# Graph attention on one Trainium2 core: another start for the first two graphs, and the second group's row statistics on ScalarE

## The chip, the cores and the metric

The kernel runs on one core of a Trainium2 chip. Five engines of that core work side by side: TensorE (PE, matrix products; its weight loads are shown apart as PEld), VectorE (DVE), ScalarE (ACT), GpSimd (POOL) and SyncE (SP, which issues nearly all DMA transfers). Each engine carries out its own list of instructions strictly in order, and engines wait for one another through semaphores. The metric is device time in microseconds for the whole computation, the median over several runs; lower is better.

## The reference, cut to what matters

The inputs are 128 graphs of 128 nodes with 768 features, one 128x128 adjacency matrix for each graph, and three 768x768 weights. Everything is float32.

```python
h = relu(layernorm(x))                                  # over the 768 features
q, k, v = (split_heads(h @ W + b) for W, b in ...)      # 12 heads of 64
s = q @ k.T / 8 + beta * adj
s = where(adj > 0, s, -9e15)
x = x + merge_heads(softmax(s) @ v)
```

## The kernel before, in words

The function `direct` treats the graphs in 32 groups of four (`GRP`); `G` is the group and `g` the graph in it. Before the products of a group, each graph's x is normalised and transposed, so that the features lie on the partitions. The weights of all three projections stay in SBUF and are cut into three slices: `qk0` (queries and keys of heads 0 to 5), `v`, and `qk1` (heads 6 to 11).

**Products.** A slice of a group is one 2x3x3 block product made with 15 instead of 18 block products (`PRODUCTS`, `product`, L320 to L363). Sums of activation blocks (`sum_acts`, L283) and of weight blocks (`sum_weights`, L197) are made by VectorE. The 15 products are spread over four PSUM banks, the chains a, b, c and d; a product adds onto what its bank holds, so the next product of a chain may start only when the last one has been read out. The first product that reaches a result is read out by ScalarE (L357) for `qk` slices, and by VectorE (L347) for `v`; every later one is added by VectorE (L361, L352). Products 0, 2, 6, 9 and 12 are on chain c, 1, 5, 10 and 13 on chain a, 3, 7, 11 and 14 on chain b, and 4 and 8 on chain d.

**Order.** Work of other kinds (the scores, the weighted sums, the next group's preparation) is put between the products by lists `todo`, whose entries `then(n, f)` are called behind the n-th product. A scheduler then sets the final place of every instruction on its engine, and `tc.issue_after` keeps an instruction behind another one. The engines run in exactly the order that results.

**Preparing a group.** The usual way lays x out so that VectorE's 32x32 transposes (`to_hT`, L275) yield the feature blocks. Statistics: VectorE makes mean and variance of each 192-wide quarter row (`stats`, L230); in `moments_1` (L235) two small TensorE products sum the quarters' means over partitions and VectorE takes deviations; in `moments_2` (L251) two more such products (L255) sum the variances, VectorE adds the constant (L258, L260), and POOL takes the inverse root (L262) and the shift (L264). Then ScalarE normalises the sixteen quarter rows of the group one by one (`norm`, L273), and VectorE transposes them.

**Group 0** is different. Graphs 0 and 1 are loaded by rows. `rows_1` (L522) makes their row statistics on VectorE and the inverse root on POOL (L536); `rows_2` (L539) normalises three pieces of 256 columns on VectorE (L544), transposes each by two TensorE products with the identity (L549), and lets ScalarE move it to SBUF (L554). `WARM` products of the identity (L560) run on TensorE before that. The slice `qk0` of group 0 is made plainly with 18 block products (`plain_slice`, L485), the very first block graph by graph. Graphs 2 and 3 go the usual way in three steps (`half`, L577).

**Group 1** is prepared while the `v` slice of group 0 runs: x is loaded (L155) behind the weights of `qk1`, `stats` is called behind products 0 to 3, `moments_1` behind 5, `moments_2` behind 7, `norm` behind 10 to 13. Then comes the `qk1` slice of group 0, with the scores of heads 0 to 5 (L382) behind its product 1, their exponentials (L389) and the transposes of group 1 (L280).

## Time and profile before

| what | value |
|---|---|
| median of four runs | 2892.67 us (2892.52 to 2893.04) |
| the profiled execution's own time | 2892.54 us |
| its span, first to last instruction | 2890.8 us |
| TensorE busy | 2879.6 us, 100% of the span |
| VectorE, ScalarE, POOL busy | 1962.1, 801.9 and 371.5 us |
| the chain that ended last | 98% TensorE |

All times inside the span count from its first instruction. A row of the timeline gives the start, the length, the engine, the line, the operation, what is written and read, the shapes and how many instructions are merged; behind it, in brackets, stands how long the engine sat idle and what ended that. TensorE's rows are pipelined: products that are 379 ns long start closer together than that, so the space between starts tells what one costs.

### The profile page before, as it was taken

How to read it: one execution, taken by the hardware profiler on the slowest of the kernel's cores; microseconds unless marked ns; L12 is line 12 of the kernel's file. 1: busy time of each engine (PE TensorE's matmuls, PEld its weight loads, DVE VectorE, ACT ScalarE, POOL GpSimd, SP SyncE). 2: the span in 40 equal slices, each digit the busy share in tenths (PEclk: the TensorE clock that was granted, in tenths of full speed). 3: DMA queues.
4: the chain of work that ended last, by engine and by line, in shares of the span. 5: the costliest groups of instructions: out<-in, count | busy, mean ns of one | idle time of the engine just before them, and what ended most of it. 6: DMA issues, size and time to landing. Idle time of an engine off the chain costs nothing.

```text
span 2890.8 us, 81358 instructions
## 1 busy us (share of the span) xinstructions
PE 2879.6 (100%) x35562; PEld 2021.3 (70%) x35562; DVE 1962.1 (68%) x4743; ACT 801.9 (28%) x1750; POOL 371.5 (13%) x304
## 2 busy tenths in 40 slices
PE   9999999999999999999999999999999999999999
PEld 7666677666677676776667766777666777666766
DVE  7876667676676666767667776667666676666765
ACT  2432322222222323223232232322223222322221
POOL 1111111111111111111111111111111111111110
PEclk9999999999999999999999999999999999999999
DMA  6322122221122111221112212122221222111211
GB/s 166 78 56 57 38 62 71 60 56 43 55 71 64 52 52 46 71 68 51 56 42 68 71 52 60 39 63 71 55 61 39 58 71 61 56 47 47 67 41 39
DMA packets 357784, 172.16 MB, mean 60 GB/s; under 512 B 84400, under 2 KB 357040, under 8 KB 357424
## 3 DMA queue, kind: packets, MB, share of 16 engines
q1 hardware_dynamic: 355552, 166.53, 21.1%
q8 instruction: 279, 4.57, 0.7%
q10 hardware_dynamic: 1872, 0.40, 0.1%
q14 instruction: 81, 0.66, 0.1%
HBM read 116.53 MB, written 50.33 MB: 58 GB/s over the span
## 4 chain that ended last, share of the span: by engine, by line
PE 98%; issue 1%; DVE 1%; POOL 0%; ACT 0%; DMA 0%; SPq 0%; ACTq 0%; POOLq 0%; DVEq 0%
PE bank L336 84%; PE bank L417 6%; PE bank L382 6%; PE bank L498 1%; PE bank L560 0%; ACT x L273 0%; POOL rstd L262 0%; DMA x<-in_x_dram 0%; DVE S L286 0%; DVE qk L361 0%; PE bank L241 0%; PE bank L255 0%; PE bank L437 0%; DVE qk_T L206 0%; PE bank L454 0%
## 5 line engine op out<-in xcount | busy, mean ns | idle before, releaser
L336 PE MATMUL bank<-S,qk_T 128*64 128x256 f32 x7056 | 822.5, 379 | 0.9 <-ACT qk L357 0.8
L336 PEld LDWEIGHTS bank<-S,qk_T 128*64 128x64 f32 x7056 | 503.6, 137 | 256.8 <-issue 4.0
L361 DVE TENSOR_TENSOR qk<-qk,bank 128x512 f32<-128x512 f32 x630 | 428.9, 681 | 340.1 <-PE bank L336 337.2
L357 ACT ACTIVATE qk<-bank,bqk 128x256 f32<-128x256 f32 x756 | 312.2, 472 | 1009.5 <-PE bank L336 778.4
L336 PE MATMUL bank<-A,qk_T 128*64 128x256 f32 x4032 | 478.6, 379 | 0.9 <-DVE qk L361 0.9
L336 PE MATMUL bank<-S,qk_B 128*64 128x256 f32 x4032 | 478.2, 379 | 1.0 <-DVE qk L361 1.0
L422 POOL TENSOR_TENSOR xo<-xo,o 128x512 f32<-128x512 f32 x189 | 252.6, 1336 | 1599.2 <-DVE o L401 1364.1
L336 PE MATMUL bank<-v_T,S 128*64 128x256 f32 x3584 | 422.6, 380 | 0.0
L352 DVE TENSOR_TENSOR v<-v,bank 128x512 f32<-128x512 f32 x320 | 220.1, 688 | 295.9 <-PE bank L336 295.9
L389 ACT ACTIVATE e<-e 128x512 f32<-128x512 f32 x378 | 227.3, 631 | 660.4 <-DVE e L386 660.0
L336 PEld LDWEIGHTS bank<-A,qk_T 128*64 128x64 f32 x4032 | 284.3, 137 | 137.4 <-DVE qk L361 1.1
L336 PEld LDWEIGHTS bank<-S,qk_B 128*64 128x64 f32 x4032 | 278.6, 137 | 128.9 <-DVE qk L361 1.4
L336 PEld LDWEIGHTS bank<-v_T,S 128*64 128x64 f32 x3584 | 252.2, 137 | 126.3 <-issue 5.7
L273 ACT ACTIVATE x<-x,shift,rstd 128x192 f32<-128x192 f32 x504 | 224.3, 533 | 350.2 <-POOL shift L264 350.2
L336 PE MATMUL bank<-v_B,S 128*64 128x256 f32 x2048 | 244.1, 380 | 0.0
L386 DVE SCALAR_TENSOR_TENSOR e<-bank,biasT 128x512 f32<-128x512 f32 x378 | 231.3, 681 | 16.7 <-PE bank L382 16.7
L336 PE MATMUL bank<-v_T,A 128*64 128x256 f32 x2048 | 237.9, 379 | 0.0
L417 PEld LDWEIGHTS bank<-v,e 128*64 128x64 f32 x6048 | 208.6, 138 | 27.3
L280 DVE STREAM_TRANSPOSE A<-x 128x256 f32<-128x256 f32 x378 | 211.9, 612 | 4.0 <-ACT x L273 4.0
L417 PE MATMUL bank<-v,e 128*64 128x65 f32 x6048 | 208.3, 221 | 0.0
L347 DVE TENSOR_TENSOR v<-bv_b,bank 128x512 f32<-128x512 f32 x192 | 131.9, 687 | 111.9 <-PE bank L336 111.9
L230 DVE BATCH_NORM_STATS2 st<-x 128x6 f32<-128x192 f32 x504 | 154.4, 344 | 75.5 <-DMA x<-in_x_dram 75.5
(83 smaller groups left out, 1689.6 us busy)
## 6 DMA issues: line engine op xcount, KB each, us to landing
x<-in_x_dram SPq DMA_DIRECT2D x504, 96.0 KB, 2.5
xo<-in_x_dram SPq DMA_DIRECT2D x189, 256.0 KB, 2.9
out_dram<-xo SPq DMA_DIRECT2D x189, 256.0 KB, 2.4
adj<-in_adj_dram SPq DMA_DIRECT2D x128, 64.0 KB, 2.4
qk_T<-in_L_gnn_Wq_dram SPq DMA_DIRECT2D x10, 128.0 KB, 3.8
qk_T<-in_L_gnn_Wk_dram SPq DMA_DIRECT2D x10, 128.0 KB, 3.8
v_T<-in_L_gnn_Wv_dram SPq DMA_DIRECT2D x5, 256.0 KB, 6.1
qk_B<-in_L_gnn_Wq_dram SPq DMA_DIRECT2D x8, 128.0 KB, 3.5
```

Source lines behind the costliest of these rows:

```text
L230: nc.vector.bn_stats(st[G][:, g * NB + b, :], xg[G, g][:, b, :])
L273: nc.scalar.activation(t, t, AF.Relu, bias=shift[G, n], scale=rstd[G, n])
L280: last = nc.vector.transpose(t[:, :, g * N:(g + 1) * N].rearrange("p c (b i) -> p c b i", i=SQ), src)
L336: nc.tensor.matmul(p[q:q + HD, i, :], lhs[:, q:q + HD], rhs, start=(first and i == 0 and c == 0), stop=(c == 1), skip_group_check=True)
L352: added[G] = nc.vector.tensor_tensor(o, o, got, ALU.add if sign > 0 else ALU.subtract)
L357: nc.scalar.activation(t[:, i, :], p[:, i, :], AF.Identity, bias=bqk[:, i, oc:oc + 1], scale=float(sign))
L361: added[G] = nc.vector.tensor_tensor(t, t, p, ALU.add if sign > 0 else ALU.subtract)
L382: nc.tensor.matmul(ps[oc, i][k:k + HD, g * N:(g + 1) * N], t[r, 1, at][:, k:k + HD], t[r, 0, at], start=True, stop=True)
L386: taken[0] = nc.vector.scalar_tensor_tensor(e, ps[oc, i].rearrange("p (g n) -> p g n", g=GRP), SCORE_CAP * ISCALE, biasT[G], op0=ALU.min, ...
L389: nc.scalar.activation(e, e, AF.Exp, scale=1.0 / ISCALE)
L417: nc.tensor.matmul(pa[q:q + HD, 2 * g + i, :], es[G, oc, i][:, 2 * r + g, q:q + HD], vt[G, "v", r, h // 4][:, 4 * g + h % 4, :], start=Tru ...
L422: nc.gpsimd.tensor_add(t, t, o.rearrange("p a (b j) d -> p (a b) (j d)", j=2))
```

## The change

Three things change, all of them at the start of the kernel.

*Graphs 0 and 1.* `rows_1` and `rows_2` are replaced by `begin` and `transposed`. On VectorE the second graph's statistics now stand between the first graph's pieces, one by one. On TensorE a fixed order is written out by `line` and `PIECES`: the transposes of a piece stand just ahead of the products that need it, or one piece earlier, and this for both graphs. `WARM` stays 18. On POOL, the scaling of `beta_c` and a memset now stand ahead of the second graph's inverse root.

*Statistics of group 1.* In place of `stats` on VectorE, `stats_by_act` has ScalarE go over each quarter row twice: a copy with a sum output gives the mean, a square with the mean as bias and a sum output gives the variance. It works on graphs 0 and 1 (called behind product 8 of the plain slice) and then on graphs 2 and 3 (called behind product 0 of the `v` slice). The first-half entries are then copied for `moments_1`, which reads two halves. The four `norm` calls are asked for one product earlier.

*Loads.* x of the first two graphs of group 1 is loaded ahead of the `qk1` weights, and not behind them.

In the order that results, ScalarE has its 32 passes between the read-outs of the plain slice and up to the normalising of group 1, and the square of `adjT` (L311) now stands ahead of that normalising. On TensorE the two small products of `moments_1` move from the middle of product 10 of the `v` slice to behind half of product 12, and those of `moments_2` from behind the first instruction pair of product 12 to behind the first pair of product 14. VectorE loses sixteen statistics instructions in that slice; from its last sum of the slice on, its order is the same as before.

```diff
--- before.py
+++ after.py
@@ -228,6 +228,25 @@
             st[G] = stat.tile([P, GRP * NB, nc.vector.BN_STATS_DIM], F32, tag="st", name=f"st_{G}", bufs=2)
         for b in range(NB):
             nc.vector.bn_stats(st[G][:, g * NB + b, :], xg[G, g][:, b, :])
+    def stats_by_act(G, lo, hi):
+        if G not in st:
+            st[G] = stat.tile([P, GRP * NB, nc.vector.BN_STATS_DIM], F32, tag="st", name=f"st_{G}", bufs=2)
+        m = stat.tile([P, hi - lo], F32, tag=f"mean{lo}", name=f"mean_{G}_{lo}", bufs=1)
+        for step in range(2):
+            for n in range(lo, hi):
+                junk = work.tile([P, QD], F32, tag="e", name=f"junk_{G}_{step}_{n}", bufs=6)
+                t = xg[G, n // NB][:, n % NB, :]
+                if step:
+                    nc.scalar.activation(junk, t, AF.Square, bias=m[:, n - lo:n - lo + 1], scale=math.sqrt(0.5),
+                                         accum_out=st[G][:, n, 2:3])
+                else:
+                    nc.scalar.activation(junk, t, AF.Copy, scale=1.0 / QD, accum_out=st[G][:, n, 1:2])
+            if not step:
+                nc.scalar.activation(m, st[G][:, lo:hi, 1], AF.Copy, scale=-math.sqrt(0.5))
+        nc.scalar.copy(st[G][:, lo:hi, 4:6], st[G][:, lo:hi, 1:3])
     def halves(G, lo, hi, n):
         return st[G].rearrange("p b (h m) -> p b h m", h=2)[:, lo:hi, :, n]
@@ -491,27 +510,28 @@
                 p = bank.rearrange("p (i w) -> p i w", i=2)
                 parts = (slice(0, N), slice(N, H2)) if r == j == 0 else (slice(0, H2),)
-                for at, k in [(at, k) for at in parts for k in range(3)]:
-                    a, b = A[G, f"A{r}{k}"], wt[sl, f"B{k}{j}"]
-                    for i in range(2):
-                        for c in range(2):
-                            last = nc.tensor.matmul(p[:, i, at], b[:, c, i * P:(i + 1) * P], a[:, c, at],
-                                                    start=(k == 0 and i == 0 and c == 0), stop=(c == 1),
-                                                    skip_group_check=True)
-                    if at is not parts[-1]:
-                        if k == 2:
-                            with tc.issue_after(last.ins):
-                                second()
-                        continue
-                    if k == 2:
-                        t = qk[G, sl, r, j] = work.tile([P, 2, H2], F32, tag="qk", name=f"{sl}_{G}_{r}_{j}", bufs=8)
-                        oc = j + 3 * int(sl[2])
+                for g, at in enumerate(parts):
+                    for k in range(3):
+                        if len(parts) == 2:
+                            for piece in PIECES[g, k]:
+                                transposed(*piece)
+                        a, b = A[G, f"A{r}{k}"], wt[sl, f"B{k}{j}"]
                         for i in range(2):
-                            nc.scalar.activation(t[:, i, :], p[:, i, :], AF.Identity, bias=bqk[:, i, oc:oc + 1])
-                        give(bank)
-                    for f in todo.get(n, ()):
-                        f()
-                    n += 1
+                            for c in range(2):
+                                line("pe", nc.tensor.matmul, p[:, i, at], b[:, c, i * P:(i + 1) * P], a[:, c, at],
+                                     start=(k == 0 and i == 0 and c == 0), stop=(c == 1), skip_group_check=True)
+                        if g == len(parts) - 1 and k < 2:
+                            for f in todo.get(n, ()):
+                                f()
+                            n += 1
+                t = qk[G, sl, r, j] = work.tile([P, 2, H2], F32, tag="qk", name=f"{sl}_{G}_{r}_{j}", bufs=8)
+                oc = j + 3 * int(sl[2])
+                for i in range(2):
+                    nc.scalar.activation(t[:, i, :], p[:, i, :], AF.Identity, bias=bqk[:, i, oc:oc + 1])
+                give(bank)
+                for f in todo.get(n, ()):
+                    f()
+                n += 1
     adj_0 = load_adj(0)
@@ -519,60 +539,83 @@
     load_weights("v", AS_SUMMED)
     first = {}
-    def rows_1(g):
-        t = xg[0, g].rearrange("p b f -> p (b f)")
-        s = stat.tile([P, 2, nc.vector.BN_STATS_DIM], F32, tag="strow", name=f"strow_{g}", bufs=2)
-        for h in range(2):
-            with ExitStack() as behind:
-                if g:
-                    behind.enter_context(tc.issue_after(first["ve"].ins))
-                nc.vector.bn_stats(s[:, h, :], t[:, h * VH:(h + 1) * VH])
-        mv = stat.tile([P, nc.vector.BN_AGGR_DIM], F32, tag="mvrow", name=f"mvrow_{g}", bufs=2)
-        nc.vector.bn_aggr(mv, s)
-        ve = stat.tile([P, 1], F32, tag="verow", name=f"verow_{g}", bufs=2)
-        first["ve"] = nc.vector.tensor_scalar(ve, mv[:, 1:2], EPS, None, op0=ALU.add)
-        r = stat.tile([P, 1], F32, tag="rsrow", name=f"rsrow_{g}", bufs=2)
-        nc.gpsimd.tensor_tensor(r, ve, nhalf, ALU.pow)
-        return mv, r
-    def rows_2(g, mv, r):
-        v = xg[0, g].rearrange("p b (j c) -> p c (b j)", c=NC)
+    def line(engine, f, *args, **kwargs):
+        with ExitStack() as behind:
+            if engine in first:
+                behind.enter_context(tc.issue_after(first[engine].ins))
+            first[engine] = f(*args, **kwargs)
+        return first[engine]
+    PIECES = {(0, 0): ((0, 0), (0, 1)), (0, 1): ((0, 2),), (0, 2): (), (1, 0): ((1, 0), (1, 1)), (1, 1): ((1, 2),),
+              (1, 2): ()}
+    rows = {}
+    def transposed(g, k):
+        bank = take()
+        p = bank[:, 0:H2].rearrange("p (c i) -> p c i", c=2)
+        for c in range(2):
+            line("pe", nc.tensor.transpose, p[:, c, :], rows[g, k][:, c, :], ident)
+        name = f"A0{k}"
+        if not g:
+            A[0, name] = work.tile([P, 2, H2], F32, tag=name, name=f"{name}_0", bufs=1 + (k > 0))
+        nc.scalar.activation(A[0, name][:, :, g * N:(g + 1) * N], p, AF.Relu)
+        give(bank)
+    def begin():
+        st, mv, r = {}, {}, {}
+        for g in range(2):
+            st[g] = stat.tile([P, 2, nc.vector.BN_STATS_DIM], F32, tag="strow", name=f"strow_{g}", bufs=2)
+            mv[g] = stat.tile([P, nc.vector.BN_AGGR_DIM], F32, tag="mvrow", name=f"mvrow_{g}", bufs=2)
+        def stats_of(g, h):
+            t = xg[0, g].rearrange("p b f -> p (b f)")
+            line("dve", nc.vector.bn_stats, st[g][:, h, :], t[:, h * VH:(h + 1) * VH])
+        def root(g):
+            line("dve", nc.vector.bn_aggr, mv[g], st[g])
+            ve = stat.tile([P, 1], F32, tag="verow", name=f"verow_{g}", bufs=2)
+            line("dve", nc.vector.tensor_scalar, ve, mv[g][:, 1:2], EPS, None, op0=ALU.add)
+            r[g] = stat.tile([P, 1], F32, tag="rsrow", name=f"rsrow_{g}", bufs=2)
+            nc.gpsimd.tensor_tensor(r[g], ve, nhalf, ALU.pow)
+        def piece(g, k):
+            v = xg[0, g].rearrange("p b (j c) -> p c (b j)", c=NC)
+            n = rows[g, k] = work.tile([P, 2, P], F32, tag="e", name=f"rows_{g}_{k}", bufs=6)
+            line("dve", nc.vector.tensor_scalar, n, v[:, 2 * k:2 * k + 2], mv[g][:, 0:1], r[g], op0=ALU.subtract,
+                 op1=ALU.mult)
+        stats_of(0, 0)
+        stats_of(0, 1)
+        root(0)
+        stats_of(1, 0)
+        piece(0, 0)
+        stats_of(1, 1)
+        piece(0, 1)
+        root(1)
+        piece(0, 2)
         for k in range(3):
-            n = work.tile([P, 2, P], F32, tag="e", name=f"rows_{g}_{k}", bufs=6)
-            first["dve"] = nc.vector.tensor_scalar(n, v[:, 2 * k:2 * k + 2], mv[:, 0:1], r, op0=ALU.subtract,
-                                                   op1=ALU.mult)
-            bank = take()
-            p = bank[:, 0:H2].rearrange("p (c i) -> p c i", c=2)
-            for c in range(2):
-                nc.tensor.transpose(p[:, c, :], n[:, c, :], ident)
-            name = f"A0{k}"
-            if not g:
-                A[0, name] = work.tile([P, 2, H2], F32, tag=name, name=f"{name}_0", bufs=1 + (k > 0))
-            t = A[0, name][:, :, g * N:(g + 1) * N]
-            nc.scalar.activation(t, p, AF.Relu)
-            give(bank)
+            piece(1, k)
     warm = take()
     for n in range(WARM):
-        nc.tensor.matmul(warm[:, 0:P], ident, ident, start=True, stop=True)
+        line("pe", nc.tensor.matmul, warm[:, 0:P], ident, ident, start=True, stop=True)
     give(warm)
-    got = [rows_1(g) for g in range(2)]
-    rows_2(0, *got[0])
-    def second():
-        rows_2(1, *got[1])
-        nc.gpsimd.tensor_scalar(beta_c, beta_c, ISCALE, None, op0=ALU.mult)
-        fold = const.tile([P, SQ], F32, name="fold")
-        nc.vector.tensor_reduce(fold, ident.rearrange("p (a i) -> p i a", i=SQ), AX.X, ALU.add)
-        nc.vector.tensor_scalar(mean8, fold[:, None, :].to_broadcast([P, NB, SQ]), -0.125, None, op0=ALU.mult)
-        for v in vring:
-            nc.gpsimd.memset(v[:, :, HD:VE], 1.0)
+    begin()
+    nc.gpsimd.tensor_scalar(beta_c, beta_c, ISCALE, None, op0=ALU.mult)
+    fold = const.tile([P, SQ], F32, name="fold")
+    line("dve", nc.vector.tensor_reduce, fold, ident.rearrange("p (a i) -> p i a", i=SQ), AX.X, ALU.add)
+    line("dve", nc.vector.tensor_scalar, mean8, fold[:, None, :].to_broadcast([P, NB, SQ]), -0.125, None,
+         op0=ALU.mult)
+    for v in vring:
+        nc.gpsimd.memset(v[:, :, HD:VE], 1.0)
     def half(step):
@@ -588,6 +631,11 @@
             for k in range(3):
                 first["dve"] = to_hT(0, 1, k)
+    def behind_product(f, *args):
+        with tc.issue_after(first["pe"].ins):
+            return f(*args)
     def behind_rows(f, *args):
         with tc.issue_after(first["dve"].ins):
@@ -620,16 +668,22 @@
         if G + 1 < NG:
             for g in range(GRP):
-                then(6, lambda g=g: load_x(G + 1, g, (nc.sync,)))
+                if G:
+                    then(6, lambda g=g: load_x(G + 1, g, (nc.sync,)))
                 if G == 1:
                     then(11 + g, lambda g=g: behind_scores(stats, G + 1, g))
                 elif G:
                     then(11 + g, lambda g=g: stats(G + 1, g))
         if not G:
+            for g in range(2):
+                load_x(1, g, (nc.sync,))
             load_weights("qk1", AS_SUMMED)
+            for g in range(2, GRP):
+                then(6, lambda g=g: load_x(1, g, (nc.sync,)))
+            then(8, lambda: stats_by_act(1, 0, 2 * NB))
             then(0, lambda: behind_rows(half, 0))
-            then(3, lambda: half(1))
-            then(4, lambda: half(2))
+            then(3, lambda: behind_product(half, 1))
+            then(4, lambda: behind_product(half, 2))
             for n in range(len(SUMS_A)):
                 then(n + 5, lambda n=n: after(sum_acts, 0, n))
             for n in range(len(SUMS_B)):
@@ -645,10 +699,10 @@
         if G + 1 < NG:
             got = []
             at = 3 if G else 5
+            if not G:
+                then(0, lambda: stats_by_act(1, 2 * NB, 4 * NB))
             for g in range(GRP):
-                if not G:
-                    then(g, lambda g=g: stats(G + 1, g))
-                then(at + 5 + g, lambda g=g: norm(G + 1, g))
+                then(at + (5 if G else 4) + g, lambda g=g: norm(G + 1, g))
             then(at, lambda: got.extend(moments_1(G + 1, 0, GRP * NB)))
             then(at + (3 if G else 2), lambda: moments_2(G + 1, 0, GRP * NB, *got[:2]))
             if G:
```

## The prediction

> **What bounds the kernel now.** I read the page first. TensorE fills the span, so an edit can only pay or cost where TensorE waits or gets more work.
>
> ```profile
> PE 2879.6 (100%) x35562; PEld 2021.3 (70%) x35562; DVE 1962.1 (68%) x4743; ACT 801.9 (28%) x1750; POOL 371.5 (13%) x304
> ```
>
> So I asked next for the waits over the whole run. The reader is to see five in all: the start, three around the seam of group 0 (0.8 and twice some 1 us), two in the tail.
>
> ```profile
> PE bank L560 <- POOL ident masks.py:199: 2.2, 1, 2.2
> PE bank L336 <- DVE qk L361: 1.9, 2, 1.0
> PE bank L698 <- DVE over L696: 1.0, 1, 1.0
> PE bank L454 <- ACT e L444: 0.9, 2, 0.6
> PE bank L336 <- ACT qk L357: 0.8, 1, 0.8
> ```
>
> The timeline shows the three at the seam and the chain that feeds the first: inverse root, normalising, then the read-out (L357) behind it on ScalarE's queue, which product 2 of `qk1` waits for. VectorE causes the other two.
>
> ```profile
> 65.82 2.91 POOL L262 TENSOR_TENSOR rstd<-ve,nhalf 128x16 f32<-128x16 f32 x1 [42.65 <-DVE ve L260]
> ...
> 69.28 7.12 ACT L273 ACTIVATE x<-x,shift,rstd 128x192 f32<-128x192 f32 x16 [25.05 <-POOL shift L264]
> ...
> 73.53 2.85 PE L382 MATMUL bank<-qk 64*64 64x128 f32 x96
> 77.17 3.67 PE L336 MATMUL bank<-S,qk_T 128*64 128x256 f32 x32 [0.79 <-ACT qk L357]
> ...
> 98.37 1.95 PE L336 MATMUL bank<-A,qk_T 128*64 128x256 f32 x16 [0.91 <-DVE qk L361]
> 101.31 1.95 PE L336 MATMUL bank<-S,qk_B 128*64 128x256 f32 x16 [0.99 <-DVE qk L361]
> ```
>
> By starts of products, these three cost 1.03, 1.08 and 1.16 us.
>
> **The change part by part.**
>
> *Graphs 0 and 1 on VectorE.* The first piece waits for POOL's root (6.67 + 0.56 = 7.23) and starts near 7.3, not at 8.11. That buys nothing: TensorE is in the `WARM` products until 9.16, and these stay.
>
> ```profile
> 2.15 7.17 PE L560 MATMUL bank<-ident 128*128 128x128 f32 x36 [2.15 <-POOL ident masks.py:199]
> 9.16 0.82 PE L549 MATMUL bank<-ident,rows 128*128 128x128 f32 x6
> 10.01 2.94 PE L498 MATMUL bank<-A,qk_T 128*128 128x128 f32 x24
> 12.80 0.82 PE L549 MATMUL bank<-ident,rows 128*128 128x128 f32 x6
> 13.65 2.94 PE L498 MATMUL bank<-A,qk_T 128*128 128x128 f32 x24
> ```
>
> The second graph's root stands behind two POOL rows (0.40 and 0.74 us) and a later variance: about 9.1 to 9.9, pieces by 11.3, needed at 13. Hidden.
>
> *Graphs 0 and 1 on TensorE.* Before, products begin 0.85 us behind the first transpose (9.16 to 10.01, 12.80 to 13.65): the transpose's latency and ScalarE's 0.39. All six transpose instructions (0.11 each) lie inside that. Now only four do; two stand behind the first products, where TensorE has no gap: 2 x 0.11 = 0.22 a graph, **+0.44** for both. If the products waited for something shorter, the least is 0; I see no gain.
>
> *Loads.* Eight issues of 0.47 to 0.75 us on SP push the 18 `qk1` weight issues 3.8 to 6 us later. They were issued at 27 to 38, are first summed at 45.9 and last near 69: the last would land near 47. Hidden; if not, VectorE's sums wait. x of graphs 2 and 3 is issued behind them, near 43 to 47, landing near 49.5, as now.
>
> *Statistics on ScalarE.* 16 VectorE instructions of 344 ns, 0.26 apart, leave the `v` slice: 4.2 us. There VectorE waits for TensorE anyway (L347, 1.6 us), so it is cover, not gain. ScalarE gets 32 passes over 192 columns with a sum. No row shows a sum output. Nearest below: the normalising, 532 ns and 0.44 apart; a small 64-column row adds 0.20 a step, so 0.64; twice 0.44 is 0.88, the upper end; the lower end is 0.36, the step of the 256-column read-out. Eight lie in the gaps 33.9 to 38.2 and 39.1 to 43.4; the other 24 run from about 44.9. At 0.55, which I take for being nearest to the normalising row plus part of a small one, with 0.75 for small copies, they end near 59 (x of graph 3 is in time). `moments_1` needs them at 65.6, so up to 0.82 a step is free; at 0.88, 1.4 us late. Queued among the passes are the read-outs of the plain slice; their banks are next used by the `v` slice after 45 and the scores at 74, so some tenths cost nothing. The square of `adjT`, now ahead of the normalising (0.63 us), has its input near 68.4 and ScalarE is free until 74: nothing.
>
> The Trainium skill, "ScalarE: Activation LUTs", section "Rules for kernel authors", sends multiplying and adding to VectorE, against this part. By its section "What ACT_TABLE_LOAD costs", a copy would step at 0.25 and a square with pointer bias at 0.35 us, with no figure for the sum: my estimate is 9.6 us plus that, against 4.2 us on VectorE. Both hide, so the rule would not alter the sum.
>
> *The moments come later: this is the main term.* In TensorE's fixed order the first pair of small products moves two products of the slice back, and so does the second (they start at 61.62 and 64.63 now). A product lasts 1.73 us (starts 60.60 less 43.29, by ten), so 3.45 us, plus 0.44 from above: the second pair lies near 68.5. VectorE's sum of variances (L258) then stands behind the read-out of product 13 and one weight sum (0.60 a step): the row ends near 70.4, against 65.74 now. POOL's root takes 2.91, shift 0.43, sixteen normalisings 7.03 at 0.44 a step, two read-outs 0.8: product 2 can start near **81.8**, against 77.17. TensorE without that wait would be there at 76.6. So the first wait grows from 1.03 to about **5.2 us**, and TensorE runs 4.67 us late.
>
> What of it comes back: VectorE keeps its order. It reached the read-out of product 3 (L361) at 82.72, while TensorE had finished that at 80.9. Now that finish is at 81.84 + 3.73 = 85.57, so VectorE idles there and runs 85.63 - 82.72 = 2.91 late. TensorE, 4.67 late, no longer waits at 98.37, and at 101.31 only until VectorE's 101.26 + 2.91. Behind that no wait takes anything back. **+2.9 us** at the end, 0.44 included. Its bounds: 1.9 if the two rows on VectorE that POOL's sums slow down (1.77 and 1.22 us) fall apart from them and other links shrink a little, 4.3 with late statistics.
>
> *TensorE's clock.* The trace starts and ends with a slow clock. The first 27 identity products start 213 ns apart, later ones 111: 27 x 0.102 = 2.75 us lost until 8.1. At the end the granted clock is halved; in the table by stages it is the number third from the end, and the columns are stage, length, busy time of each engine, clock, DMA share and GB/s:
>
> ```profile
> 2882.26:2885.67 3.41, 2.20 (x49) 1.61 (x48) 3.20 (x15) 1.51 (x4) 0.00 (x0) 1.00 0.29 80
> 2885.67:2889.08 3.41, 0.21 (x2) 0.09 (x2) 1.33 (x6) 0.00 (x0) 0.00 (x0) 1.00 0.29 87
> 2889.08:2890.80 1.72, 0.00 (x0) 0.00 (x0) 0.00 (x0) 0.00 (x0) 0.00 (x0) 0.50 0.01 5
> ```
>
> That is 2.6 us behind the last product's end (2886.50). The waits now, 1.2 us at most, never do it (nine tenths or more in all forty slices of the page). The new wait leaves TensorE without work from 76.9 to 81.8, nearly twice 2.6 us, so I expect the clock to drop there. The price lies between 0 and 2.75 us; I take **2.1**, near the only restore that the trace has, and below it since the clock is down for part of the wait already. While it is slow, VectorE waits with TensorE for product 3, so the loss adds on.
>
> The Trainium skill, "TensorE: Matmul & The Clock Gate", section "What's actually happening", says that the clock halves after an idle window of about 3.4 us that runs freely, and comes back after a busy one. It speaks against this change. By it, a wait of 4.9 us holds a full window in (4.9 - 3.4)/3.4, or 44%, of the phases, and the price is 1.4 to 3 us, varying from run to run; my estimate of the sum by the page alone is 2.9 or about 5.0.
>
> *Sum.* 2.9 + 2.1 = 5.0 on the profiled execution's 2892.54: 2897.5. That one stands 0.13 below the median 2892.67, so 2897.7 for the median.
>
> **The rivals.**
>
> 1. *The clock holds:* same wait, no slow products: 2892.67 + 2.9 = 2895.6. For it: no wait in the middle of the run shows a drop.
> 2. *Slower by over 0.2%: ScalarE's statistics end late.* TensorE's first small product waits for them, and everything behind shifts. It decides at 0.82 us a pass; each 0.1 beyond adds 2.4 us. At 0.88 it is 2892.67 + 5.0 + 1.4 = 2899.1. The dearest clock price (2.75 + 2.9 = 5.65) also comes near the bound. Against it: 0.44 for the same width without a sum.
> 3. *Faster: the two VectorE waits go and the first one stays as it is.* VectorE would have to be a microsecond ahead at 82.7, with product 2 starting before 78.9. Price: -2.24 + 0.44, or 2890.9. Against it: the order puts the moments two products later, and 0.3 + 2.9 + 0.4 + 7.0 + 0.8 us of POOL and ScalarE follow them.
> 4. *The root and normalising do not hold product 2* (another cause for the 0.79 us): only 0.44 is left, 2893.1. Against it: ScalarE's read-out ends at 77.12 and TensorE starts at 77.17.
>
> **How the numbers follow.** 0.2% is 5.8 us, about what a measurement of this kernel can tell from no change; the bounds are 2886.9 and 2898.5. Chances: forecast 0.58 (2896.4 to 2898.6), rival 1 0.24 (2894.6 to 2896.4), rival 2 0.10, rival 3 0.04, rival 4 0.04. Rival 3 by itself stays within the bounds, and all three waits sum to 3.3 us, so under 2886.9 I leave 0.02, for what no row shows. Slower: most of rival 2 and a fifth of the forecast, 0.21. Same: 0.77. The range leaves out rivals 3 and 4 and the far end of 2: 2894.2 to 2899.8.
>
> **What would show it.** Right: the wait before product 2 of `qk1` at about 5 us, named after ScalarE's read-out; L262 starting near 70.5; L273 near 74; no wait at VectorE's read-out of product 9; products of 128x256 at twice their spacing behind the long wait and a granted clock under 1. The passes of `stats_by_act` end before 65. First products at 10.01 and near 13.87. Wrong: L262 before 66, a first wait near 1 us, or small products waiting for ScalarE's sums.

## The result, and the profile after

The changed kernel takes **2897.25 us** (median; 2895.39 to 2898.44 over 40 runs), the kernel before 2892.65 us (2891.56 to 2893.83 over 60). The ratio is **1.0015**, with a 95% interval of 1.0011 to 1.0020: 4.6 us slower, well shown though it lies within the 0.2% named above. The forecast was 2897.7. The profiled execution's own time is 2896.76 us, its span 2895.0. The changed kernel's times spread over 3.1 us, those of before over 2.3 although there were more of them; one source of such a spread is shown in the last section.

The waits of TensorE in the changed kernel, those at its beginning and at the seam (columns: who waits for whom, us in total, times, longest):

```profile
PE bank L355 <- ACT qk L376: 4.8, 1, 4.8
PE bank L547 <- POOL ident masks.py:199: 2.2, 1, 2.2
...
PE bank L355 <- DVE qk L380: 0.6, 2, 0.4
PE bank L547 <- DVE rows L547: 0.4, 1, 0.4
PE bank L547 <- ACT A L564: 0.3, 1, 0.3
```

The wait before product 2 of `qk1` has grown from 0.8 to 4.8 us, and the waits on VectorE's read-outs have shrunk from 1.9 to 0.6. The timeline of the changed kernel shows the start, two passes of ScalarE's statistics, and then the chain that feeds this wait (line numbers have moved: the start of TensorE is L547, the passes L246, products L355, scores L401, root L281, shift L283, normalising L292, read-out by ScalarE L376, by VectorE L380):

```profile
2.16 5.98 PE L547 MATMUL bank<-ident 128*128 128x128 f32 x36 [2.16 <-POOL ident masks.py:199]
...
8.87 0.44 PE L547 MATMUL bank<-ident,rows 128*128 128x128 f32 x2 [0.44 <-DVE rows L547]
9.15 1.06 PE L547 MATMUL bank<-A,qk_T 128*128 128x128 f32 x8
...
15.90 1.89 PE L547 MATMUL bank<-A,qk_B 128*128 128x256 f32 x8
...
35.84 0.35 ACT L246 ACTIVATE junk<-x 128x192 f32<-128x192 f32 x1
36.09 0.19 ACT L246 ACTIVATION_READ_ACCUMULATOR junk<-x 128x1 f32 x1
36.19 0.35 ACT L246 ACTIVATE junk<-x 128x192 f32<-128x192 f32 x1
...
69.50 2.90 POOL L281 TENSOR_TENSOR rstd<-ve,nhalf 128x16 f32<-128x16 f32 x1 [46.89 <-DVE ve L279]
72.48 0.22 POOL L283 TENSOR_TENSOR shift<-mean,rstd 128x16 f32<-128x16 f32 x1
...
72.74 7.12 ACT L292 ACTIVATE x<-x,shift,rstd 128x192 f32<-128x192 f32 x16 [4.71 <-POOL shift L283]
79.77 1.53 ACT L376 ACTIVATE qk<-bank,bqk 128x256 f32<-128x256 f32 x4
...
72.94 2.85 PE L401 MATMUL bank<-qk 64*64 64x128 f32 x96
80.63 5.36 PE L355 MATMUL bank<-S,qk_T 128*64 128x256 f32 x32 [4.84 <-ACT qk L376]
85.82 1.90 PE L355 MATMUL bank<-S,qk_B 128*64 128x256 f32 x16
...
86.11 0.69 DVE L380 TENSOR_TENSOR qk<-qk,bank 128x512 f32<-128x512 f32 x1 [4.06 <-PE bank L355]
...
102.43 1.90 PE L355 MATMUL bank<-A,qk_T 128*64 128x256 f32 x16
104.74 1.95 PE L355 MATMUL bank<-S,qk_B 128*64 128x256 f32 x16 [0.41 <-DVE qk L380]
```

What to see: the 36 identity products, unchanged, took 5.98 us and not 7.17 as in the trace of before; the next block of products starts at 15.90, earlier than the 16.43 of before, and the `v` slice at 42.74 for 43.29. That gain is mostly this execution's early clock and not the new start: in experiment 2 the old start, with an early clock, reaches the `v` slice at 42.77. A pass of ScalarE with a sum has a row of its own for reading the accumulator. At the seam, root, shift, normalising and read-out follow each other without a gap from 69.50 on, and product 2 starts at 80.63, behind the first read-out. Products 2 and 3 then take 5.36 us where the same 32 instructions took 3.67 before. VectorE sits idle for 4.06 us until product 3 is done. The wait that stood at 98.37 is gone, and of the one at 101.31 a part is left at 104.74.

The clock in this execution, in a table by stages whose edges are the moments at which it changes, and one and two such steps before (columns as above: stage, length, busy time of PE, PEld, DVE, ACT and POOL, granted clock, DMA share, GB/s):

```profile
74.01:77.42 3.41, 1.78 (x68) 1.54 (x58) 3.34 (x6) 3.41 (x9) 0.00 (x0) 1.00 0.02 5
77.42:80.83 3.41, 0.20 (x2) 0.20 (x4) 3.41 (x7) 3.41 (x9) 0.00 (x0) 1.00 0.00 0
80.83:84.25 3.42, 3.42 (x18) 1.95 (x16) 1.22 (x3) 3.42 (x8) 0.00 (x0) 0.50 0.00 0
84.25:87.66 3.41, 3.41 (x34) 2.27 (x32) 1.55 (x3) 0.89 (x3) 0.00 (x0) 1.00 0.00 0
```

The clock halves at the end of a stage in which TensorE was busy for 0.20 of 3.41 us, and is back one stage later. Products 2 and 3 lost 5.36 - 3.67 = 1.69 us by it here.

### The profile page after: what moved, and what is told of

Read it like the earlier page. It is cut to its first block, busy times and chain, and to the rows that moved or that the text cites. A ratio compares the mean times of both kernels' runs of the same rounds, so it can differ in the third digit from the quotient of the medians.

```text
span 2895.0 us, 81404 instructions
## 1 busy us (share of the span) xinstructions
PE 2880.4 (99%) x35562; PEld 2020.7 (70%) x35562; DVE 1958.5 (68%) x4727; ACT 815.9 (28%) x1818; POOL 370.8 (13%) x304
## 4 chain that ended last, share of the span: by engine, by line
PE 95%; issue 2%; DVE 2%; DMA 0%; POOL 0%; ACT 0%; SPq 0%; ACTq 0%; POOLq 0%; DVEq 0%
PE bank L355 82%; PE bank L401 6%; PE bank L436 6%; PE bank L547 1%; DMA x<-in_x_dram 0%; DVE S L305 0%; POOL rstd L281 0%; DVE qk L380 0%; ACT x L292 0%; DVE qk_T L206 0%; DVE A L299 0%; POOL xo L441 0%; PE bank L260 0%; PE bank L274 0%; PE bank L456 0%
## 5 line engine op out<-in xcount | busy, mean ns | idle before, releaser
L355 PE MATMUL bank<-S,qk_T 128*64 128x256 f32 x7056 | 824.4, 380 | 5.2 <-ACT qk L376 4.8
L355 PEld LDWEIGHTS bank<-S,qk_T 128*64 128x64 f32 x7056 | 504.1, 137 | 262.8 <-issue 5.6
L380 DVE TENSOR_TENSOR qk<-qk,bank 128x512 f32<-128x512 f32 x630 | 428.9, 681 | 341.2 <-PE bank L355 337.3
L376 ACT ACTIVATE qk<-bank,bqk 128x256 f32<-128x256 f32 x756 | 312.1, 472 | 1008.2 <-PE bank L355 776.7
L355 PE MATMUL bank<-S,qk_B 128*64 128x256 f32 x4032 | 478.2, 379 | 0.4 <-DVE qk L380 0.4
L355 PE MATMUL bank<-A,qk_T 128*64 128x256 f32 x4032 | 478.5, 379 | 0.0
L355 PE MATMUL bank<-v_T,S 128*64 128x256 f32 x3584 | 422.4, 380 | 0.0
L355 PEld LDWEIGHTS bank<-A,qk_T 128*64 128x64 f32 x4032 | 284.3, 137 | 136.5 <-issue 0.2
L355 PEld LDWEIGHTS bank<-S,qk_B 128*64 128x64 f32 x4032 | 278.5, 137 | 128.4 <-DVE qk L380 0.9
L355 PEld LDWEIGHTS bank<-v_T,S 128*64 128x64 f32 x3584 | 251.9, 137 | 126.2 <-issue 5.7
L292 ACT ACTIVATE x<-x,shift,rstd 128x192 f32<-128x192 f32 x504 | 224.3, 533 | 329.5 <-POOL shift L283 329.5
L355 PE MATMUL bank<-v_B,S 128*64 128x256 f32 x2048 | 243.7, 380 | 0.0
L355 PE MATMUL bank<-v_T,A 128*64 128x256 f32 x2048 | 237.5, 379 | 0.0
```

What stands on the lines that cost most here:

```text
L292: nc.scalar.activation(t, t, AF.Relu, bias=shift[G, n], scale=rstd[G, n])
L355: nc.tensor.matmul(p[q:q + HD, i, :], lhs[:, q:q + HD], rhs, start=(first and i == 0 and c == 0), stop=(c == 1), skip_group_check=True)
L376: nc.scalar.activation(t[:, i, :], p[:, i, :], AF.Identity, bias=bqk[:, i, oc:oc + 1], scale=float(sign))
L380: added[G] = nc.vector.tensor_tensor(t, t, p, ALU.add if sign > 0 else ALU.subtract)
```

## The experiments

Theory: the small products of the moments lie later, this stretches the wait before product 2, and in it the clock drops. Rivals: ScalarE's passes or the loads cost by themselves; the new start costs, or gains; the clock costs nothing, since VectorE is the bound there.

**1. The new start alone.** `stats_by_act` and the early loads taken out of the changed kernel.

```diff
-            then(8, lambda: stats_by_act(1, 0, 2 * NB))
...
-                then(0, lambda: stats_by_act(1, 2 * NB, 4 * NB))
+                    then(g, lambda g=g: stats(G + 1, g))
-                then(at + (5 if G else 4) + g, lambda g=g: norm(G + 1, g))
+                then(at + 5 + g, lambda g=g: norm(G + 1, g))
```

> Only the new start of graphs 0 and 1; the second group's statistics stay on VectorE and the loads stay where they were. Theory (the late moments are the cause): nearly nothing, 2892.65 + 0.44 for the transposes that lie outside the latency = 2893.1, up to 2893.7 because the second pair of small products still falls 0.65 us later; the wait before product 2 of qk1 stays near 1 to 1.7 us and the granted clock stays at 1.00 in it. Rival 'the new start costs the time': 2895 or more. Rival 'the new start gains' (rows are there earlier): under 2892.3.

Measured: 2893.76 us for 2892.46 of the kernel before beside it, ratio 1.0004 (0.9995 to 1.0013).

```profile
77.40 3.67 PE L355 MATMUL bank<-S,qk_T 128*64 128x256 f32 x32 [0.33 <-ACT qk L376]
```

The wait before product 2 has not grown (0.33 us idle, 0.79 before), and its products run at the full clock. The median lies just above the theory's upper edge, all eleven times (2892.97 to 2894.30) lie above the median of before, and yet the interval holds no change, so the size of this part isn't settled; it is not where 4.6 us went.

**2. The statistics on ScalarE alone.** The kernel before with `stats_by_act`, the early loads and the earlier `norm` calls.

> Only ScalarE's statistics and the earlier loads; the start is that of before. Theory: nearly all of the loss: the small products lie two products later as in the changed kernel, the wait before product 2 is about 5 us, the clock halves in it, and the time is 2892.65 + 4.05 (first wait 5.08 for 1.03) + 1.65 (slow clock) - 1.08 - 0.59 (the two later waits shrink) = 2896.7. Rival 'the start costs': 2893 or less.

Measured: 2896.84 us, ratio 1.0015 (1.0006 to 1.0024). Its timeline on TensorE:

```profile
80.69 5.10 PE L355 MATMUL bank<-S,qk_T 128*64 128x256 f32 x32 [4.67 <-ACT qk L376]
...
104.55 1.73 PE L355 MATMUL bank<-S,qk_B 128*64 128x256 f32 x14 [0.42 <-DVE qk L380]
```

The same wait, the same slow products (5.10 for 3.67, so 1.43 us), the same rest at product 13: this part carries the loss, as expected to 0.2 us. The two parts measured alone, 1.3 and 4.4 us, are more than the 4.6 of both together; the intervals of single runs, some 2.6 us to either side, leave room for that.

**3. The moments early again.** The changed kernel with TensorE's order fixed by hand from the `v` slice to product 2 of `qk1`.

```diff
+    def pin(on, *args, **kwargs):
+        with ExitStack() as behind:
+            if on and pinned:
+                behind.enter_context(tc.issue_after(pinned["pe"].ins))
...
-            then(at, lambda: got.extend(moments_1(G + 1, 0, GRP * NB)))
-            then(at + (3 if G else 2), lambda: moments_2(G + 1, 0, GRP * NB, *got[:2]))
+            then(at if G else 9, lambda: got.extend(moments_1(G + 1, 0, GRP * NB)))
+            then(at + 3 if G else 11, lambda: moments_2(G + 1, 0, GRP * NB, *got[:2]))
```

> The changed kernel with TensorE's order pinned, so that the small products of the moments stand ahead of products 10 and 12 of the v slice again, the matrix of biases made behind them, and the normalising with two read-outs as before. ScalarE still makes the statistics in 32 passes and the start is the new one. Theory (only the place of the moments costs): the row of POOL's root starts near 66.3 instead of 69.5, the wait before product 2 is 1 to 1.6 us, the clock stays at 1.00, the time 2892.65 + 0.44 + 0.2 = 2893.3 (2892.7 to 2893.9). Rival 'the passes on ScalarE or the loads cost by themselves': 2895.5 to 2897.3, as the changed kernel.

Measured: 2892.11 us, ratio 0.9999 (0.9990 to 1.0008). All 32 passes are still on ScalarE and the loads are still early, and the loss is gone: the rival that these cost by themselves falls. Two stages and two rows of its trace:

```profile
74.39:77.80 3.41, 1.68 (x44) 1.22 (x38) 3.41 (x7) 3.41 (x10) 0.00 (x0) 1.00 0.02 5
77.80:81.21 3.41, 3.41 (x34) 2.27 (x32) 3.41 (x8) 3.41 (x7) 0.00 (x0) 1.00 0.00 0
```

```profile
65.41 2.90 POOL L291 TENSOR_TENSOR rstd<-ve,nhalf 128x16 f32<-128x16 f32 x1 [42.79 <-DVE ve L289]
...
77.07 3.67 PE L257 MATMUL bank<-S,qk_T 128*64 128x256 f32 x32 [1.73 <-ACT qk L386]
```

The root starts at 65.41, not at the 66.3 that I had expected; product 2 starts at 77.07 (before: 77.17), with a longer wait only because TensorE came to it earlier. A stage half busy (1.68 of 3.41 us) did not halve the clock.

**4 and 5. The wait filled.** Products of the identity, into a free bank, behind the scores, so that TensorE is busy while product 2 waits: first 32 calls, then 18.

```diff
+        if G == u == 0:
+            for n in range(32):
+                with tc.issue_after(last.ins):
+                    last = nc.tensor.matmul(free[0][:, 0:P], ident, ident, start=True, stop=True)
```

> The changed kernel with 32 products of the identity (0.11 us each) put on TensorE between the scores and product 2 of qk1, into a bank that is free then. Nothing else waits for them; they end near 79.5, before product 2 can start. Theory: the first wait's end stays at 80.6, but the clock does not halve; products 2 and 3 take 3.7 instead of 5.4 us, and the whole 1.65 us comes off: 2897.25 - 1.65 = 2895.6 (2895.2 to 2896.0), and the times lie closer together. Rival 'the slow stretch is hidden by VectorE, which is the bound there': no change, 2897.0 to 2897.4. Rival 'the clock halves all the same': no change, with a clock of 0.5 in the profile.

Measured: 2897.85 us, ratio 1.0019 (1.0010 to 1.0028), a miss by my own sizing. A call is two instructions of 0.11 us:

```profile
75.50 7.41 PE L412 MATMUL bank<-ident 128*128 128x128 f32 x64
82.84 3.67 PE L355 MATMUL bank<-S,qk_T 128*64 128x256 f32 x32
```

The filling ended 2.2 us too late. Even so, product 2 starting 2.21 us later costs only 0.6 us, near the 2.21 - 1.69 = 0.52 that a full clock would leave. But the filling changed more than TensorE's work: the scheduler also put VectorE's instructions behind it into another order. The read-out of product 3 stands behind thirteen instructions there that follow it in the changed kernel, and starts at 89.32, though product 3 ended at 86.51. So the agreement proves little.

> As the filled wait before, with 18 products of the identity in place of 32. The last run showed that one such product costs 0.22 us and not 0.11, so its 32 ended at 82.8 and held product 2 back themselves; 18 take 4.0 us and end near 79.6, before product 2 can start at 80.6. Theory (the clock halves because TensorE is idle, and costs 1.65 us): full clock throughout, products 2 and 3 in 3.7 us, 2897.25 - 1.65 = 2895.6 (2895.1 to 2896.1). Rival (the slow stretch is hidden by VectorE): 2897.0 to 2897.5.

Measured: 2895.38 us, ratio 1.0011 (1.0002 to 1.0020), within the theory's range.

```profile
75.78 4.29 PE L412 MATMUL bank<-ident 128*128 128x128 f32 x36
80.70 3.67 PE L355 MATMUL bank<-S,qk_T 128*64 128x256 f32 x32 [0.63 <-ACT qk L376]
...
86.60 0.69 DVE L380 TENSOR_TENSOR qk<-qk,bank 128x512 f32<-128x512 f32 x1
```

Product 2 starts where it did in the changed kernel, and it and product 3 take 3.67 us: with TensorE kept busy the clock does not drop. The 2897.25 - 2895.38 = 1.9 us between the medians are not the clock's price alone, though. VectorE's order has changed here too: it reads product 3 at 86.60, behind eight other instructions, though that product ended at 84.37; in the changed kernel it stood idle for it.

The price can be read where VectorE's order in the `qk1` slice is the same: in the traces of experiment 2, of the changed kernel, and of experiment 8 below. Counted from the start of the `v` slice, product 13 begins at 58.02 us before the change, and in these three at 61.78, 62.00 and 62.25, so 3.76, 3.98 and 4.23 late. Products 2 and 3 lost 1.43, 1.69 and 1.97 us of that to the clock, and what is left is 2.33, 2.29 and 2.26. So the clock's price, **1.4 to 2.0 us**, arrives at product 13 nearly in full, and the late start of product 2 costs **2.3**. The rival that VectorE hides the slow stretch falls by this.

The two make 4.0 us, and the medians differ by 4.6. From 114 us to the end the profiled execution of the changed kernel goes from 3.42 to 4.21 us behind that of before. It does so in four jumps (+0.26, -0.12, +0.23 and +0.42, at 818.6, 1444.5, 1712.8 and 2606.8 us of before), where both kernels do the same work. The traces of experiments 3 and 6, whose kernels take as long as before, jump at such places too, by up to 0.36. What makes these jumps, and whether they are the 0.6 us that the medians have more, no run shows; kernels without the loss have them too.

**6. The read-out first.** Nothing but ScalarE's order is changed: the read-out of product 0 stands ahead of the sixteen normalisings, and the square behind them. The moments stay late.

```diff
+            for g in range(GRP):
+                then(0, lambda g=g: behind_read(norm, 1, g))
...
-            then(5, lambda: square(early[0]))
+            then(5, lambda: behind_norm(square, early[0]))
```

> The changed kernel with one thing moved on ScalarE: the read-out of product 0 of the first qk1 slice stands ahead of the sixteen normalisings and not behind them (and the square of the bias matrix behind them). The moments stay as late as they are. Theory (product 2 is held only by the read-out that queues behind the normalising): product 2 starts at 75.8, right behind the scores, with no wait and a full clock; VectorE is at its read-out of product 3 at 82.0 as it was before the wait there, and no longer idles; what is left are the two later waits on VectorE. Time 2892.65 - 0.7 (82.0 for 82.72) + 0.2 = 2892.1 (2891.6 to 2892.9). Rival (the late normalising holds VectorE's transposes, and so TensorE, anyway): 2894.5 to 2897.

Measured: 2892.54 us, ratio 0.9999 (0.9990 to 1.0008).

```profile
71.32 0.84 ACT L376 ACTIVATE qk<-bank,bqk 128x256 f32<-128x256 f32 x2 [14.86 <-PE bank L355]
72.73 7.12 ACT L292 ACTIVATE x<-x,shift,rstd 128x192 f32<-128x192 f32 x16 [0.57 <-POOL shift L283]
...
72.94 2.85 PE L401 MATMUL bank<-qk 64*64 64x128 f32 x96
75.72 3.67 PE L355 MATMUL bank<-S,qk_T 128*64 128x256 f32 x32
...
97.73 1.95 PE L355 MATMUL bank<-A,qk_T 128*64 128x256 f32 x16 [0.82 <-DVE qk L380]
100.68 1.95 PE L355 MATMUL bank<-S,qk_B 128*64 128x256 f32 x16 [1.00 <-DVE qk L380]
```

The normalising starts as late as in the changed kernel (72.73), and the whole loss is gone. The orders of TensorE and of VectorE up to the end of the slice are those of the changed kernel. So the late moments cost only through the place of one read-out in ScalarE's queue, and the rival that the normalising was not what held product 2 falls too. VectorE reads product 3 at 82.06, as expected. What bounds then is VectorE: product 2 starts 1.45 us earlier than in the kernel before, product 13 only 0.63 (100.68 for 101.31), and of that 0.55 is the early start of this execution.

**7. The moments halfway.** The kernel of experiment 3 with the small products ahead of products 11 and 13.

> The kernel of moments_early with the small products one product later (ahead of products 11 and 13 of the v slice), halfway between it and the changed kernel. Theory: root near 67.3, normalising from 71, product 2 at 78.9, a wait of 3.5 us; VectorE is at product 3's read-out at 82.0 and TensorE ends it at 82.6, so nearly all of the longer wait is taken back: 2892.1 to 2892.9 if the clock holds, which is the likelier case in this short a wait, and up to 1.5 us more in those executions in which it halves. Rival (each microsecond that the moments are late costs one): 2892.11 + 1.8 = 2893.9 with a full clock.

Measured: 2895.37 us, ratio 1.0009 (1.0000 to 1.0018), times from 2893.43 to 2897.01. Above both expectations: the wait became 4.03 us by starts, not 3.5, since the root started at 68.44 and not at 67.3; and the clock did halve.

```profile
76.32:79.73 3.41, 0.00 (x0) 0.00 (x0) 3.41 (x8) 3.41 (x9) 0.00 (x0) 1.00 0.02 5
79.73:83.15 3.42, 3.15 (x16) 1.82 (x18) 2.76 (x6) 3.42 (x8) 0.00 (x0) 0.50 0.00 0
```

Products 2 and 3 take 5.21 us here, 1.54 too many. So the cost isn't proportional to the lateness: 1.97 us of wait are free (experiment 3), 4.03 cost 2.8 us (with an interval that reaches down to no change) and 5.08 cost 4.6.

**8. The changed kernel once more**, for another phase of the clock.

> The changed kernel itself, unaltered, for a second profile in another phase of the clock. Theory: the clock changes only at multiples of 3.413 us from its first rise, so the halving falls on another moment of the wait, between 77.5 and 81; where it falls early, the next stretch of 3.4 us is mostly idle too and stays slow, so the price differs from the first profile's 1.65 us. Times between 2895.4 and 2898.4 with a median near 2897.2. Rival (the price is the same in each execution): products 2 and 3 take 5.36 us again and times lie within 1 us.

Measured: 2897.06 us, times from 2894.91 to 2899.30, a wider spread than I had named.

```profile
74.34:77.75 3.41, 1.38 (x52) 1.14 (x44) 3.41 (x7) 3.41 (x9) 0.00 (x0) 1.00 0.03 5
77.75:81.16 3.41, 0.60 (x4) 0.41 (x6) 3.41 (x7) 3.41 (x10) 0.00 (x0) 0.50 0.00 0
81.16:84.58 3.42, 3.42 (x20) 1.90 (x18) 0.82 (x2) 3.42 (x8) 0.00 (x0) 0.50 0.00 0
```

```profile
80.56 5.64 PE L355 MATMUL bank<-S,qk_T 128*64 128x256 f32 x32 [4.84 <-ACT qk L376]
```

The wait is the same, 4.84 us. But the steps fall elsewhere: the clock halves at 77.75, already in the middle of the wait, behind a stage that was busy for 1.38 us; the next stage is busy for 0.60 and doesn't restore it; a full one does. Price 5.64 - 3.67 = 1.97 us.

**9 to 11. A version that beats both.** In the `v` slice the changed kernel leaves VectorE room (it waits there for TensorE), and in the `qk1` slice VectorE holds TensorE. So: the start of before, ScalarE's statistics, the moments early, the read-out first, and seven of the nine `qk0` weight sums moved into the `v` slice; then also the bias matrix of group 1 kept behind product 13; then the same with the changed kernel's start.

```diff
+                for n in range(7):
+                    then(2 * n + 1, lambda n=n: behind_adds(sum_weights, "qk0", n))
...
-            for n in range(9):
+            for n in range(7, 9):
                 then(n + 2, lambda n=n: behind_scores(sum_weights, "qk0", n))
```

> A version meant to beat both: the start of before, ScalarE's statistics, the small products ahead of products 10 and 12 of the v slice, the read-out of product 0 ahead of the normalising, and seven of the nine sums of qk0 weights moved by VectorE from the qk1 slice into the v slice, where the 16 statistics instructions have left it 4.2 us idle. Theory: all three waits of TensorE at the seam go (1.03, 1.08, 1.16 us): 2892.65 - 3.27 = 2889.4 (2889.0 to 2890.2). Rival (the sums hold up VectorE's read-outs in the v slice, or other work of VectorE in the qk1 slice is the limit): 2891 to 2893.

Measured: 2891.45 us, ratio 0.9996 (0.9987 to 1.0005): a miss of 2 us, and not clear of no change. Two of the three waits at the seam are gone, the middle one has grown from 1.08 to 1.51 us by starts:

```profile
90.78 0.70 DVE L328 STREAM_TRANSPOSE adjT<-adj 128x512 f32<-128x512 f32 x1
91.52 0.43 DVE L330 TENSOR_SCALAR kp<-adjT 128x512 uint8<-128x512 f32 x1
...
92.46 0.48 DVE L331 TENSOR_SCALAR adjT<-adjT,beta_c 128x512 f32<-128x512 f32 x1
93.04 0.75 DVE L334 COPY_PREDICATED biasT<-kp,adjT 128x512 f32<-128x512 uint8 x1
...
97.90 1.95 PE L257 MATMUL bank<-A,qk_T 128*64 128x256 f32 x16 [1.34 <-DVE qk L390]
```

Four rows that nobody needs before the next group had moved up into the room that was made, ahead of the read-outs.

```diff
-            then(13, lambda: early.append(behind_scores(bias_1, 1, load_adj(1))))
+            then(13, lambda: early.append(behind_adds(bias_1, 1, load_adj(1))))
```

> sums_moved with the bias matrix of group 1 (four rows on VectorE, 2.0 us together, which had moved up between 90.8 and 93.8 once the sums were gone) kept behind the read-out of product 13. Theory: the last wait of TensorE at the seam (1.51 us, on VectorE's read-out before product 12) goes: 2891.45 - 1.5 = 2890.0 (2889.3 to 2890.7). Rival (another row of VectorE takes its place): 2891 to 2892.

Measured: **2889.44 us**, ratio 0.9989 (0.9980 to 0.9998). No wait of over 0.3 us is left on TensorE between 9 and 140 us:

```profile
96.04 1.90 PE L257 MATMUL bank<-A,qk_T 128*64 128x256 f32 x16
97.77 1.90 PE L257 MATMUL bank<-S,qk_B 128*64 128x256 f32 x16
```

> bias_later with the changed kernel's start of graphs 0 and 1. The traces so far show that the clock first rises anywhere between 5.0 and 8.2 us, and that the v slice then starts at 42.5 to 42.8 with the new start when it rises by 6.4, and at 43.3 to 43.6 when it rises after 7.4; with the old start it is 42.8 to 43.3 whatever the clock. Theory (the new start gains up to 0.6 in early rises and loses 0.4 in late ones): within 0.3 us of bias_later. Rival (the transposes cost 0.44 in every execution, as predicted): 0.4 us above bias_later or more.

Measured: **2889.30 us**, ratio 0.9988 (0.9979 to 0.9997). Both are 3.3 to 3.5 us under the kernel before, and the two starts can't be told apart: within the 0.3 us of the theory, and against the rival as far as eleven runs of each can tell 0.4 us.

## Why the prediction was right

The verdict and the time were right (2897.7 for 2897.25, +5.0 for +4.6), and the runs bear out the mechanism: the late moments, the wait, and the clock in it. That the number came so near is in part luck, as the end of this section says. By its steps:

- **The moments later.** Right. The forecast put root, first normalising and product 2 at 70.5, near 74 and 81.8; the trace has 69.50, 72.74 and 80.63. All are about 1.1 us early, of which 0.99 is the start: the sum let the `v` slice begin at 43.29 + 0.44 = 43.73, and it began at 42.74. Counted from there, product 2 was due at 38.07 and came at 37.89. The wait was forecast at 5.2 and is 5.08 us.
- **What comes back.** Right in kind and place: VectorE waits at product 3, the wait at 98.37 is gone, a rest of the last one stays, and nothing later gives anything back. Forecast 2.9 us without the clock, 0.44 of it for the start, so 2.5 for the late moments; the three traces under experiment 5 say 2.3.
- **The clock.** Forecast 2.1 us; 1.43, 1.54, 1.69 and 1.97 in the four profiles that have such a wait, 1.7 in the mean, so right in kind and 0.4 too dear. The chances were not right: rival 1 (the clock holds) had 0.24, and no profile with a wait of over 4 us showed it. What the prediction held for it, nine tenths in all forty slices of the page, could not have shown a drop, since the page of the changed kernel has nines in all forty too: 3.41 us at half clock take 2% off a slice of 72 us.
- **When the clock drops.** The estimate that only a wholly idle stage of 3.41 us counts, and so 44% of the phases, was wrong: at the seam a stage with TensorE busy for 1.38 us of it (40%) was enough, while 1.68 and 1.78 (49% and 52%) were not. Behind the first rise, every stage of the thirteen traces with 1.65 us or less of work in it was followed by a halved clock. Busy time alone is not the whole rule: near the end of experiment 2's trace a stage with 2.00 us (59%) was followed by one too. An idle time of 4.84 us leaves some stage at most 1.0 us of work (6.83 - 4.84 = 1.99, halved), so at this wait the drop should have been taken as near certain. The section "What's actually happening" of the Trainium skill's "TensorE: Matmul & The Clock Gate" speaks of an idle window; the traces decide, and here the window need not be idle all through.
- **Graphs 0 and 1 on VectorE**, "buys nothing: TensorE is in the `WARM` products until 9.16". This failed as a general step. 9.16 was one execution's phase. The 36 identity products take 7.17 us in the trace of before, 5.98 in that of the changed kernel, 5.68 in that of experiment 2, as the clock rises at some moment between 5.0 and 8.2 us. Where it rises early, the rows set the start, and the new order has its first row at 7.07 to 7.44 in the traces where the old order has it at 7.91 to 8.49.
- **The +0.44 of the transposes.** It shows, in part, where the clock rises late: the `v` slice starts at 43.33 to 43.62 in the three traces of the new order with a rise behind 7.4 us, for 43.29 before (rise at 8.23). Where the clock rises by 6.4, the earlier rows outweigh it: 42.52 to 42.81 in six traces, for 42.77 to 43.34 in three of the old order. Over eleven runs each the two orders about cancel (experiments 10 and 11); experiment 1, at 1.3 us above before, speaks against that and isn't settled. So this term should have been near 0.
- **Statistics on ScalarE.** Hidden, as forecast, and cheaper: 0.35 us a step for the copy and 0.44 for the square where I took 0.55, finished at 56.3 and not 59, needed at 64.39. The term's size was wrong and cost nothing, since it was covered. "It is cover, not gain" was right for this kernel; the last kernels use that room and, with the read-out moved as well, come out 3.3 us under the kernel before.
- **The loads.** Hidden, as forecast. Graphs 2 and 3 of group 1 set the start of ScalarE's second half at 48.79, long before it is needed.
- **The rivals.** 2 (statistics late): they ended 8 us early. 3 (faster): its condition, product 2 before 78.9, did not come about; experiments 9 to 11 show what it takes. 4 (the normalising does not hold product 2): excluded by experiment 6.

So the sum erred the same way in three terms. At product 13 it puts TensorE 5.0 us late, and the profiled execution is 3.43 late there (104.74 for 101.31): 0.99 of the difference is the start (0.44 that did not come, 0.55 by this execution's early clock), 0.4 the clock and 0.2 the late start of product 2. That this execution ended 4.2 us late all the same comes from the 0.8 us of jumps further on, which are not in the sum. The mechanism was foreseen; that the medians lie within 0.4 us of the sum is partly luck.

## What to carry to other kernels

When work moves to another engine, look first at where the scheduler puts the small instructions that depend on it: two instruction pairs, two products later, cost more than 32 added ScalarE passes, and they cost it only because an unrelated read-out stood behind their consumer in one in-order queue. A longer wait of the busiest engine need not cost in proportion: in this place one of 1.97 us cost nothing, since another engine was the bound behind it, and those of 4 and 5 us brought a slow stretch of clock on top. Independent work put into the wait kept the clock up, but check what it does to the order on the other engines. Room won on an engine gained nothing here until the work that binds later was moved into it by hand, and the scheduler first filled the room with something else.

## What was not expected of the hardware

**The clock changes on a grid.** From its first rise to every later change lies a multiple of 3.413 us: 22 steps (75.09 us) and 1 step (3.41) in the changed kernel, 21 (71.68) and 2 (6.83) in its second profile, 844 steps (2880.85) to the end of the kernel before. The grid's phase differs from run to run: the first rise came at 5.00 to 8.23 us in thirteen traces, though the first product started at 2.15 or 2.16 in each. A stage decides that: in the trace of before, the stage from 1.41 to 4.82 has TensorE busy for 2.67 us (78%), and the clock rises only one stage later, at 8.23; in experiment 4 the stage from 1.59 to 5.00 has 2.85 us (83%), and the clock rises at its end. That moves the end of the same 36 products by 1.5 us, and it gives one wait of 4.84 us two prices, 1.69 and 1.97 us. So the phase can account for a part of the spread of the changed kernel's times; no run here ties a time to its phase.

**A sum output has its own row.** ScalarE's pass with a sum is followed by a row that reads the accumulator (0.19 us long, timeline of the changed kernel). It starts 0.25 us behind the copy, and the next copy 0.10 behind it: the sum adds about 0.1 us to a step. The steps of 0.25 and 0.35 us without a sum that the prediction worked out from the Trainium skill ("ScalarE: Activation LUTs", "What ACT_TABLE_LOAD costs") agree with the measured 0.35 and 0.44 less that 0.1. That page's rule to leave adding and multiplying to VectorE decided nothing here, since both places are covered.
